# A planner's rule: a group already filled past 0.9 takes no further piece that costs more than 0.9

## The chip, the cores and the metric

The kernel runs on one core of a Trainium2 chip. The metric is the device time of one execution in microseconds (us), and the time of a kernel is the median of its runs. The engines are named as the profile names them: PE multiplies matrices, PEld is PE's loading of the stationary operand, DVE and POOL do elementwise work, ACT does activations and copies, SP issues transfers in the order of the program. Each engine works through its own list of instructions in order; semaphores tie the lists together.

## The reference

One post-norm transformer layer on x of 8 batches x 1024 rows x 256 columns, in float32:

```python
Q, K, V = (split_heads(x @ W.T + b) for W, b in ...)          # 16 heads of 16
scores = Q K^T / 4 + prior_lambda * gaussian_mask             # two bells over |i - j|
x = layernorm(x + (softmax(scores) V) @ Wo.T + bo)
h = bitlinear(x, w_fc) + gate * (x @ v.T @ fast_b.T @ u.T)    # 256 -> 1024
x = layernorm(x + bitlinear(relu(h)**2, w_proj))              # 1024 -> 256
```

bitlinear rounds the weights to -1, 0 and 1 times a scale per row. The attention is full: 1024 x 1024 scores for each of 8 x 16 heads.

## The kernel before

**The main loop.** The attention is cut into 512 groups, 64 for each of the 8 batches (`for g in range(-LEAD, total + 1)`; `per_batch` is 64 and `total` is 512). A batch has 4 sets of 4 heads, a set has two halves of 512 queries, and a half is 8 groups, one for each block of 128 keys. So a pattern comes back every 16 groups, and I call g modulo 16 the position of a group. In the order of the program, group g does this:

- `exp_scores` twice (L698 on): four PE matmuls into a PSUM tile pair `e` (L714), each for one head. Where a block of keys lies near the queries, the prior's window is added to the first pair by four more PE matmuls (L724, "prior") and to the second by DVE (L737). ACT then takes the exponential (L738). `near(g)` says whether the block is near; I call groups near and far by it.
- the pieces of other work that the planner chose for this group (their PE part),
- `max_scores` for group g + 12 (L647): four PE matmuls into tiles `s`, of which DVE takes the row maximum (L659, 1.22 us each, two a group),
- the elementwise part of the chosen pieces (their `empty` functions: ACT copies, DVE and POOL work) and what was deferred to this group (`run_deferred`),
- `weigh` for group g - 1 (L753): eight PE matmuls of the exponentials by V.

The tiles `e` and `s` take turns in three PSUM slots, so a group can also be held by the chain e, exponential, s, maximum. The pieces share two halves of one PSUM bank (`misc`).

**The pieces.** `jobs_of(b)` makes for every batch one list of pieces: queries and keys of this and the next batch (`queries_keys`, L593, and the transfers `write_parts` L196 to L201), transposes of x (`transpose_x`, L540), values (`values`, L566), and the layer's rest for the batch before, in four chunks of 256 rows (`chunk`): `project` (L953, two a chunk), `turn` (L987, two), `low_rank` (L1000), `hidden` (L1027 and L1034, eight) and `output` (L1062), two output rows of tiles with two parts each. A part of an output is 8 pairs of weight loads and 128x256 matmuls. Each piece is a tuple: its cost as the planner sees it, its function, how many of the two `misc` halves it takes, and a test of whether it may run yet.

The costs are 0.22 for `transpose_x`, 0.86 for `values`, `queries_keys` and `project`, 0.23 for `turn`, 0.48 for `low_rank`, 0.6 for `hidden` and 0.93 for a part of an `output`. Part 0 of an output takes one half of the bank, and part 1 goes on in the same half.

For the very last batch `last_chunk` has the same kinds of pieces, with `project` at 1.3 (L1163); its list `own` is put behind the others from group 505 on.

**The planner.** In group g it takes pieces from the front of the list as long as one fits. A second part of an output that stands at the front of the list when a group begins is always taken first. `filled` is the cost taken so far. `spare` says how many groups are left over in this batch, by a count of the larger pieces; in the last batch, groups 448 on, it is 0.

```python
spare = left - groups_for(jobs) if g < total - per_batch else 0
while jobs and halves >= jobs[0][2] and ready(jobs[0]):
    cost = jobs[0][0]
    if g < per_batch: ...
    elif filled > 0.75 and not (spare < (-1 if near(g) else 2)):
        break
    cost, piece, room = jobs.pop(larger(jobs) if halves == 1 and g >= per_batch else 0)[:3]
    filled += cost
```

So a group filled past 0.75 takes more only where few groups are to spare. `larger` may bring a piece of 0.5 to 0.9 ahead of small ones.

**Transfers at the pieces' edges.** `fill_stack` (L298, called at every sixteenth group) copies the next set's queries and keys from DRAM into SBUF, eight transfers of 256 KB, on SP; SP's list also has the writes of `write_parts`, the rows of maxima (L684, L691) and x (L99). `normalize` and the layer norms are spread over groups by `defer`.

**The end.** After group 512 the attention's PSUM pools are closed and the remaining pieces run one after the other, each with its elementwise part at once. Two pieces `divide_last(1)` and the projections of chunks 2 and 3 are set between them by place in the list (`jobs[:1]`, `jobs[1:4]`, `jobs[4:7]`, `jobs[7:8]`, `jobs[8:]`).

Of the kernel before, what the change touches and what calls it, by code (L numbers as in the profile page):

```python
# [38 lines left out]
def tile_postln_layer(  # L39
# [263 lines left out]
    def fill_stack(G):  # L303

        assert made.get((G // NG, G % NG // 2)) == 2 * NHALF
        for pr in range(NP):
            for a in range(2):
                for name in "kq":
                    fill_one(name, G, pr, a, nc.sync)
# [20 lines left out]
    def load_later():  # L330
        nc.sync.dma_start(v_sb, v)
        nc.sync.dma_start(fb_sb, fast_b)
        nc.sync.dma_start(u_sb, u.rearrange("(c p) r -> p c r", p=P))
        nc.sync.dma_start(gate_c, gate.partition_broadcast(P))
        nc.sync.dma_start(bo_row, bo.partition_broadcast(P))
# [32 lines left out]
    def run_deferred(upto):  # L368
        due = [f for n, f in later if n <= upto]
        later[:] = [u for u in later if u[0] > upto]  # L370
        for f in due:
            f()
# [283 lines left out]
    def max_row(t, blk, out, name):  # L656

        junk = p1.tile([P, L], F32, tag="junk", name=f"junk_{name}")
        nc.vector.tensor_tensor_reduce(  # L659
            out=junk,  # L660
            in0=t.rearrange("p k n -> p (k n)"),
            in1=wide[:, LEFT - P * blk : LEFT - P * blk + L],
            scale=1.0,
            scalar=-3.0e38,
            op0=ALU.add,
            op1=ALU.max,
            accum_out=out,
        )
# [29 lines left out]
    def exp_scores(i):  # L698

        step, n = divmod(i, STEP)
        G, h = divmod(step, NHALF)
        n, pr = divmod(n, NP)
        blk = order[h][n]
        s = G % SLOTS
        t = se(f"e_{i}")
        first = blk * P - MARGIN
        lo, hi = max(first, HALF * h), min(first + WIN, HALF * (h + 1))
        near = lo < hi  # L710
        by_pe = near and pr == 0 and (hi - lo > MARGIN or G < NG)
        for a in range(2):
            rows = slice(0, P if a else P // 2 + 2)
            nc.tensor.matmul(  # L714
                t[:, a, :],
                stack["k", s, pr, a][rows, ts(blk, P)],
                stack["q", s, pr, a][rows, ts(h, HALF)],
                start=True,
                stop=not by_pe,
            )  # L720
        if by_pe:
            for a in range(2):
                for n in range(2):
                    nc.tensor.matmul(  # L724
                        t[:, a, lo - HALF * h : hi - HALF * h],
                        ident_r,
                        prior[:, n, lo - first : hi - first],
                        start=False,
                        stop=(n == 1),
                    )  # L730
        e = big(f"exp_{i}")

        def rest():
            if near and not by_pe:
                part = t[:, :, lo - HALF * h : hi - HALF * h]
                add = win[:, lo - first : hi - first].unsqueeze(1)
                nc.vector.tensor_add(part, part, add.to_broadcast([P, 2, hi - lo]))  # L737
            nc.scalar.activation(e, t.rearrange("p a n -> p (a n)"), AF.Exp)  # L738

        return e, rest  # L740
# [674 lines left out]
    def ready(u):  # L1415

        return len(u) < 4 or u[3]()

    def larger(jobs):

        for n, u in enumerate(jobs[:5]):
            if 0.5 < u[0] < 0.9 and u[2] == 1 and ready(u):
                return n
            if u[0] != 0.22:
                break
        return 0
# [9 lines left out]
    def near(g):  # L1436

        step, n = divmod(g, NB)
        h = step % NHALF
        lo, hi = order[h][n] * P - MARGIN, (order[h][n] + 1) * P + MARGIN  # L1440
        return lo < HALF * (h + 1) and hi > HALF * h

    def groups_for(jobs):

        return sum(1.0 if u[0] > 0.7 else 0.5 if u[0] > 0.5 else 0.0 for u in jobs)
# [24 lines left out]
    for g in range(-LEAD, total + 1):  # L1470

        now = g
        if g == -2:
            fill_stack(1)
            load_later()
        if 0 <= g < total and g % per_batch == 0:
            if g:
                assert not jobs
                jobs = [u for part in jobs_of(g // per_batch) for u in part]
        if g == total - 7:  # L1480

            old, jobs = jobs, []
            while old and old[0][0] > 0.1 and old[0][2] == 0:
                jobs.append(old.pop(0))
            while old:
                jobs += [own.pop(0), *old[:2]]
                old = old[2:]
            jobs, own = jobs + own, []
        if g > 0 and 2 * g % PER_G == 0 and 2 * g // PER_G + 1 < B * NG:
            fill_stack(2 * g // PER_G + 1)  # L1490
        if 0 <= g < total:
            es[g], exps = zip(*(exp_scores(i) for i in (2 * g, 2 * g + 1)))
            exps[0]()

        if rest is not None:
            max_row(*rest)
            rest = None
        if 0 <= g < total:
            exps[1]()

        halves, work, filled = 2, [], 0.0

        if g >= 0 and jobs and jobs[0][0] > 0.1 and jobs[0][2] == 0:
            filled, piece = jobs.pop(0)[:2]
            work.append(piece)
            halves -= 1

        done = g + LEAD - (1 if g < 0 else 2)
        if done >= 0 and done % QSTEP == QSTEP - 1 and done < total:
            work.append(lambda done=done: set_max(done // QSTEP))  # L1510
            halves -= 1
        if g < 0:

            n = g + LEAD + 1 - (done >= QSTEP - 1)
            upto = 14 * n // (LEAD - 1)
            if halves == 2:
                work += [early.pop(0)[1] for _ in range(len(early) - 14 + upto)]
        elif g < total:
            left = per_batch - 1 - g % per_batch
            if g == 0:  # L1520
                among = len(jobs)
            if g < per_batch:

                behind = len(jobs) > among * (1 - (g + 1) / (per_batch - 3))
            else:
# [4 lines that stand above are left out]
                if g < per_batch:  # L1530
                    if not (cost == 0.0 or behind):
                        break
                    behind = len(jobs) - 1 > among * (1 - (g + 1) / (per_batch - 3))
                elif filled > 0.75 and not (spare < (-1 if near(g) else 2)):
                    break
                cost, piece, room = jobs.pop(larger(jobs) if halves == 1 and g >= per_batch else 0)[:3]
                filled += cost
                halves -= room
                work.append(piece)
                if cost == 0.01:  # L1540
                    break
                if jobs and jobs[0][0] > 0.1 and jobs[0][2] == 0:
                    halves = 0
        empties = [piece() for piece in work] if g >= 0 else []
        if g + LEAD < total:
            pair, blk, pm = max_scores(g + LEAD)
            max_row(pair[0], blk, pm[:, 0:1], f"{g + LEAD}_0")
            if g < 0:

                empties = [piece() for piece in work]  # L1550
            rest = pair[1], blk, pm[:, 1:2], f"{g + LEAD}_1"
        for empty in empties:
            if empty is not None:
                empty()
        run_deferred(g)
        if g - 1 in es:
            weigh((g - 1) // NB, (g - 1) % NB, es.pop(g - 1))
# [82 lines left out]
```

## Time and profile before

| | |
|---|---|
| median of 3 runs | 2231.86 us (2230.23 to 2234.39) |
| profiled execution: its time | 2231.73 us |
| profiled execution: span from first to last instruction | 2229.9 us |
| PE busy | 2160.5 us, 97% |
| DVE, ACT, POOL busy | 1591.5, 1442.7, 902.7 us |
| mean granted PE clock | 0.992 |

The starts of L714's first matmul in each group cut the trace into groups. From group 128 on a group takes 3.5 to 5.6 us; a group of the same position with the same pieces mostly takes the same time within 0.02 us in batch after batch. A row of the view of stretches gives, for the time from A to B, the busy time of each engine, with the number of instructions in brackets, then the granted PE clock (1.00 is full), the share of the transfer engines, and GB/s. A PE row that is shorter than the stretch shows PE waiting. In the timeline, the bracket at the end of a line is the engine's idle time before it and what ended it.

### The profile page before, as it was taken

Reading aid. Unit: us, or ns where it says so; the run is one execution under the profiler, and the core shown is the slowest. Engines: PE = TensorE matmul, PEld = TensorE weight load, DVE = VectorE, ACT = ScalarE, POOL = GpSimd, SP = SyncE. Lnnn points to the kernel's source line nnn. Section 1 sums busy time; section 2 is a strip of 40 time slices with the busy share of each in tenths; the row PEclk is TensorE's granted clock in tenths of the full one; section 3 lists DMA queues with packets and bytes.
Section 4 is the critical chain, followed back from the end, with each engine's and each line's share of the span. In section 5 each row is a group of like instructions: output and inputs, shape, how many; then the busy total and the mean of one; then the engine's idle time right before and its main releaser. Section 6 shows DMA issues by size and latency. Waiting matters only on the chain.

```text
span 2229.9 us, 36851 instructions
## 1 busy us (share of the span) xinstructions
PE 2160.5 (97%) x13144; PEld 1258.9 (56%) x13144; DVE 1591.5 (71%) x2952; ACT 1442.7 (65%) x2155; POOL 902.7 (40%) x1024
## 2 busy tenths in 40 slices
PE   6999999999999999999999999999999999999997
PEld 3444445555555555556555555555655555555557
DVE  6777776777777776777777777677777777677736
ACT  2665566666666667666666667676666666666654
POOL 4133322445333453245533444335443345444444
PEclk8999999999999999999999999999999999999998
DMA  7433334123433224423333223421344321422010
GB/s 194 109 92 89 74 96 114 66 71 75 118 115 87 56 56 119 129 71 80 75 125 103 73 67 92 130 87 52 75 118 116 87 71 46 132 70 53 22 46 20
DMA packets 110572, 193.36 MB, mean 87 GB/s; under 512 B 21100, under 2 KB 50108, under 8 KB 110388
## 3 DMA queue, kind: packets, MB, share of 16 engines
q1 hardware_dynamic: 108972, 189.42, 30.8%
q8 instruction: 104, 1.70, 0.3%
q10 hardware_dynamic: 1416, 1.58, 0.2%
q14 instruction: 80, 0.66, 0.1%
HBM read 105.19 MB, written 85.69 MB: 86 GB/s over the span
## 4 chain that ended last, share of the span: by engine, by line
PE 82%; DVE 8%; POOL 1%; issue 1%; ACT 1%; DMA 1%; SPq 0%; POOLq 0%; DVEq 0%; ACTq 0%
PE e L714 22%; PE av L753 19%; PE s L647 15%; DVE junk L659 6%; PE e L724 5%; PE misc L1027 4%; PE misc L593 4%; PE misc L1062 4%; PE misc L953 2%; PE misc L566 2%; PE misc L1034 1%; ACT exp L738 1%; DVE st L911 1%; PE misc L987 1%; PE misc L540 0%
## 5 line engine op out<-in xcount | busy, mean ns | idle before, releaser
L659 DVE CUSTOM_DVE_ANT_0 junk<-s,wide 128x1024 f32<-128x1024 f32 x1024 | 1248.6, 1219 | 534.3 <-PE s L647 492.0
L738 ACT ACTIVATE exp<-e 128x1024 f32<-128x1024 f32 x1024 | 1027.6, 1025 | 622.4 <-PE e L724 376.3
L714 PE MATMUL e<-st_q,st_k 66*128 66x512 f32 (+1 forms) x2048 | 664.6, 425 | 0.6 <-ACT exp L738 0.3
L714 PEld LDWEIGHTS e<-st_q,st_k 66*128 66x128 f32 (+1 forms) x2048 | 324.1, 189 | 463.3 <-ACT exp L738 82.5
L753 PE MATMUL av<-exp,v 128*17 128x512 f32 x4096 | 540.8, 600 | 0.0
L647 PE MATMUL s<-st_k,st_q 64*128 64x512 f32 x2048 | 400.5, 447 | 43.7 <-DVE pm L659 26.7
L647 PEld LDWEIGHTS s<-st_k,st_q 64*128 64x128 f32 x2048 | 167.3, 185 | 179.5 <-DVE pm L659 66.7
L737 DVE TENSOR_TENSOR e<-e,wide 128x372 f32<-128x372 f32 (+2 forms) x376 | 190.8, 507 | 47.0 <-PE e L714 41.9
L1045 POOL TENSOR_TENSOR rl<-rl 128x512 f32<-128x512 f32 x112 | 116.6, 1041 | 250.8 <-ACT hi L1044 243.4
L724 PEld LDWEIGHTS e<-prior,ident_r 128*128 128x128 f32 x1056 | 159.7, 190 | 24.2
L753 PEld LDWEIGHTS av<-exp,v 128*17 128x17 f32 x4096 | 68.1, 95 | 185.6 <-issue 184.5
L724 PE MATMUL e<-prior,ident_r 128*128 128x244 f32 (+2 forms) x1056 | 157.7, 272 | 0.0
L1047 POOL TENSOR_TENSOR lo<-rl,hi 128x512 fp32r<-128x512 f32 x112 | 143.9, 1285 | 8.8
L576 POOL TENSOR_TENSOR v<-v,bv_row 128x256 f32<-128x256 f32 x64 | 43.8, 686 | 213.4 <-ACT v L575 213.4
L1082 POOL TENSOR_TENSOR r<-r,sp_row 128x256 f32<-128x256 f32 x56 | 41.2, 735 | 205.1 <-ACT r L1081 205.1
L1027 PE MATMUL misc<-xhi,wfT 128*128 128x256 f32 x448 | 116.0, 282 | 0.2 <-ACT fullq L608 0.2
L1027 PE MATMUL misc<-xlo,wfT 128*128 128x256 f32 x448 | 115.1, 280 | 0.0
L1062 PE MATMUL misc<-wpT,lo 128*128 128x256 f32 x448 | 111.7, 283 | 2.1 <-POOL lo L1047 2.1
L1062 PE MATMUL misc<-wpT,hi 128*128 128x256 f32 x448 | 113.8, 287 | 0.0
L613 POOL TENSOR_TENSOR twok<-fullk,twok 128x512 fp32r<-128x512 f32 x30 | 38.6, 1288 | 163.0 <-ACT twok L612 163.0
L1040 ACT ACTIVATE rl<-misc,s_fc 128x256 f32<-128x256 f32 x224 | 94.3, 475 | 0.2
L1062 PEld LDWEIGHTS misc<-wpT,lo 128*128 128x128 f32 x448 | 85.1, 190 | 6.3 <-POOL lo L1047 2.9
(241 smaller groups left out, 2353.8 us busy)
## 6 DMA issues: line engine op xcount, KB each, us to landing
st_k<-parts_k SPq DMA_DIRECT2D x128, 256.0 KB
st_q<-parts_q SPq DMA_DIRECT2D x124, 256.0 KB
parts_k<-twok SPq DMA_DIRECT2D x60, 512.0 KB
parts_q<-twoq SPq DMA_DIRECT2D x64, 256.0 KB
parts_q<-twoq SPq DMA_DIRECT2D x30, 512.0 KB
x<-in_L_attn_x_dram SPq DMA_DIRECT2D x16, 512.0 KB
raw_o<-avs SPq DMA_DIRECT2D x248, 32.0 KB
rec<-back SPq DMA_DIRECT2D x30, 256.0 KB
```

Source lines behind the costliest of these rows:

```text
L647: nc.tensor.matmul(pair[a][:, kh, :], stack["q", s, pr, a][rows, ts(blk, P)], stack["k", s, pr, a][rows, ts(kh, HALF)], start=True, stop=True,
L659: nc.vector.tensor_tensor_reduce(out=junk, in0=t.rearrange("p k n -> p (k n)"), in1=wide[:, LEFT - P * blk : LEFT - P * blk + L], scale=1. ...
L714: nc.tensor.matmul(t[:, a, :], stack["k", s, pr, a][rows, ts(blk, P)], stack["q", s, pr, a][rows, ts(h, HALF)], start=True, stop=not by_pe,)
L724: nc.tensor.matmul(t[:, a, lo - HALF * h : hi - HALF * h], ident_r, prior[:, n, lo - first : hi - first], start=False, stop=(n == 1),)
L737: nc.vector.tensor_add(part, part, add.to_broadcast([P, 2, hi - lo]))
L738: nc.scalar.activation(e, t.rearrange("p a n -> p (a n)"), AF.Exp)
L753: nc.tensor.matmul(av[32 * j : 32 * j + HD + 1, :], v_bufs[b % 2][:, blk, g * HG + j, : HD + 1], es[j // 2][:, ts(j % 2, HALF)], start=(n ...
L1027: nc.tensor.matmul(ph, wfT[:, dc, ts(hc, P)], st[k2][:, dc, :], start=(dc == 0 and k2 == "xhi"), stop=False,)
L1040: nc.scalar.activation(rl[:, ts(k, n)], ph, AF.Relu, scale=s_fc[:, hc : hc + 1])
L1045: nc.gpsimd.tensor_mul(rl, rl, rl)
L1047: sub(lo, rl, hi.bitcast(F32))
L1062: nc.tensor.matmul(py, st[k][:, hc, ts(i, P)], wpT[:, hc, :], start=(hc == 0 and k == "hi"), stop=(hc == NHC - 1 and k == "lo"),)
```

## The change

One condition is added to the planner's loop. It is reached where the two conditions before it did not end the loop. It ends the loop when the group is filled past 0.9, the piece at the front costs more than 0.9, and `spare` is over -4. Pieces over 0.9 are the parts of an output (0.93) and the last batch's projections (1.3).

```diff
                 elif filled > 0.75 and not (spare < (-1 if near(g) else 2)):
                     break
+                elif filled > 0.9 and cost > 0.9 and spare > -4:
+                    break
                 cost, piece, room = jobs.pop(larger(jobs) if halves == 1 and g >= per_batch else 0)[:3]
                 filled += cost
                 halves -= room
```

No instruction is added, removed or resized; pieces go to other groups. Written X for `transpose_x`, Q for `queries_keys`, V for `values`, P for `project`, T for `turn`, L for `low_rank`, H for `hidden`, O for a part of an output, M for the transpose of the maxima (`set_max`), the groups differ as follows, and all others are the same:

```
groups 137 to 151, and the same 64, 128, 192, 256 groups later (batches 2 to 6)
before  XOO XQ XQ Q  MV V V V PP XQ XQ XQ MQ XT V
after   XO  O  XQ XQ MQ V V V VP XP XQ XQ MQ XQ TV

groups 459 to 462     before  QOO O OM -      after  QO O MO O
groups 481 to 493     before  OO - TOO T ML HH HH P PH HH HO O M
                      after   O  O TO  O MT L  HH HH PP HH HH O OM
groups 507 to 511     before  PP P P TT L     after  P P P P TT
```

In the last row P costs 1.3. After group 512 the list before begins with H of chunk 0; after the change it begins with L, one piece more, so the pieces set between by place come one piece earlier: before `H | divide | H T T | divide | H H L | P P | H | P P | H H H`, after `L | divide | H H T | divide | T H H | P P | L | P P | H H H H`. From there on the order is the same.

## The prediction

> **What bounds the kernel now.** I read the page first: the busy row, the clock and the chain that ended last.
>
> ```profile
> span 2229.9 us, 36851 instructions
> PE 2160.5 (97%) x13144; PEld 1258.9 (56%) x13144; DVE 1591.5 (71%) x2952; ACT 1442.7 (65%) x2155; POOL 902.7 (40%) x1024
> PEclk8999999999999999999999999999999999999998
> PE 82%; DVE 8%; POOL 1%; issue 1%; ACT 1%; DMA 1%; SPq 0%; POOLq 0%; DVEq 0%; ACTq 0%
> ```
>
> PE is busy nearly throughout and is 82% of the chain; the clock falls only at both ends. A change that only moves PE work between groups can then win only where PE waits. So next I cut the trace into groups and looked at the view of stretches, group by group, where pieces move. In the first stretch, groups 137, 138, 140, 150 and 151:
>
> ```profile
> 615.88:620.78 4.90, 4.90 (x38) 3.33 (x34) 2.83 (x7) 3.31 (x6) 0.73 (x1) 1.00 0.12 28
> 620.78:625.09 4.31, 4.31 (x30) 2.49 (x27) 3.02 (x6) 2.85 (x5) 0.73 (x1) 1.00 0.00 0
> ...
> 628.96:633.05 4.09, 4.09 (x28) 2.32 (x25) 3.14 (x6) 2.57 (x4) 1.49 (x2) 1.00 0.96 316
> ...
> 669.84:673.76 3.92, 3.92 (x29) 2.23 (x25) 3.25 (x6) 2.88 (x5) 1.30 (x1) 1.00 0.05 12
> 673.76:677.74 3.98, 3.71 (x24) 1.89 (x20) 2.98 (x8) 2.31 (x3) 0.19 (x1) 1.00 0.69 265
> ```
>
> Full groups are PE from end to end. Group 137 with three pieces takes 4.90. The least that PE needs in a far group without pieces is about 4.90 - 2 x 0.95 - 0.22 = 2.8 (O is 8 matmuls 0.12 apart, X 0.22), and some 3.2 in a near one (4.31 less X and Q, 0.86). Group 151, with only V, should need 2.8 + 0.86 = 3.66 and takes 3.98: thin groups are held by the chain through DVE. The last batch, in groups 462, 481, 482, 483 and 493, has more of this:
>
> ```profile
> 1957.50:1961.51 4.01, 3.80 (x24) 1.74 (x20) 3.36 (x6) 2.05 (x2) 3.18 (x4) 1.00 0.03 9
> ...
> 2037.35:2042.46 5.11, 4.96 (x37) 3.20 (x33) 2.88 (x7) 3.10 (x5) 4.26 (x6) 1.00 0.61 127
> 2042.46:2046.40 3.94, 3.80 (x24) 1.74 (x20) 3.36 (x6) 2.05 (x2) 2.87 (x3) 1.00 0.00 0
> 2046.40:2051.32 4.92, 4.92 (x38) 3.34 (x34) 2.65 (x7) 2.31 (x3) 0.00 (x0) 1.00 0.01 3
> ...
> 2088.92:2092.42 3.50, 3.03 (x22) 1.25 (x18) 2.54 (x5) 2.23 (x4) 3.42 (x4) 1.00 0.00 0
> ```
>
> Groups 462 and 482 have no piece at all and still take 4.01 and 3.94, 0.7 to 0.8 over PE's need; overfull neighbours take 5.11 and 4.92. An O put into an empty near group costs little there: the view of stretches has near groups with one O at 4.18 and far ones at 3.73.
>
> **The change part by part.** No instruction is added, so I price a group by one with the same pieces at a like position.
>
> Batches 2 to 6, groups 137 to 151 each. 137 goes from XOO to XO: the nearest rows are TO far, 3.96 (group 473) and 4.06 (five groups), I take 4.03: -0.87. 138 goes from XQ 4.31 to O 4.17 (group 106): -0.14. 140 goes from Q 4.09 to XQ 4.32 (group 148): +0.23. 150 goes from XT 3.92 to XQ 4.31 (group 70): +0.39. 151 goes from V 3.98 to TV, which I put at 4.05, the XQ of group 71 at that position: +0.07. The others move by a piece but keep a like content (145 from PP to VP, 146 from XQ to XP, 4.33 in group 78): +0.01. Sum -0.31 a batch, -1.6 in five. What is won is slack of the thin groups 150 and 151. Bounds: -0.6 a batch if both lose all their slack (3.92 - 3.67 for XT and 3.98 - 3.66), and +0.25 if O in 138 or 151's T makes PE wait once for the maxima as group 135's O does (0.25). SP: the last Q of queries and keys comes one group later, in 141, so its three writes fall behind the rows of maxima (L684, L691), as they do at group 149: some 5.5 us later. That holds back `fill_stack`. The first reader is `s` of group 148. From the timeline the last issue and that reader, and from the view of stretches the end of the copies:
>
> ```profile
> 645.80 0.59 SPq L298 DMA_DIRECT2D st_q<-parts_q  x1
> ...
> 652.00:654.00 2.00, 2.00 (x14) 0.74 (x15) 1.23 (x2) 0.65 (x2) 1.43 (x2) 1.00 0.33 78
> 654.00:656.00 2.00, 2.00 (x14) 1.68 (x12) 1.90 (x3) 1.03 (x1) 0.00 (x0) 1.00 0.00 1
> ...
> 664.43 0.73 PE L647 MATMUL s<-st_k,st_q 64*128 64x512 f32 x4
> ```
>
> The transfers are over by 654, the reader comes at 664.4. The writes take 3 us (transfer engines busy from 636 to 639), so the eight copies would start at 645.5 in place of 642 and be over by 657 or 658: 6 us of cover remain, and I cost it at nothing. The x load of group 139 moves to 140, and its first use at 146 stays; 20 us lie between.
>
> Groups 459 to 462. 18.00 us before (5.56, 4.18, 4.25, 4.01). After: QO is 5.56 - 0.95 = 4.61, O near 4.18, MO 3.83 (group 93), O near 4.18: 16.80, -1.2. But the second O's layer-norm statistics (DVE 0.42 and 0.18) now fall into group 463, beside the two subtractions of TT (0.42 each), and 463 and 464 already wait for DVE. I give back 0.3 (half of the 0.6 of DVE work): -0.9, bounds -1.2 and -0.6.
>
> Groups 481 to 493. 55.07 before. After, in order: 3.73, 4.17, 4.03, 4.17, MT 3.85, L 4.15 (group 464: 4.17), 4.05, 4.05, PP 4.50, 4.39, 3.95, 4.19, OM 3.83: 53.06, -2.0. Bounds -2.5, if L's group costs 3.7, PE's need alone, and -1.4, if the statistics beside T and L cost all their 0.6.
>
> Groups 507 to 510. 16.70 before. After, each with one P: 3.80, 4.27, 3.80, 4.27 (rows of 509 and 508 before), 16.14: -0.55, while TT (0.45 on PE) goes to 511 and L out of it. In 511 the exponentials now stand ahead of TT's copies on ACT (0.37 each), so the last of them ends some 0.5 us sooner. Bounds -1.0 and 0.
>
> The end. From the start of group 511 the list began after 5.8 us, with H. Now it begins with L after some 5.1. Before, H H L stood between the last divide and P P, and L waited 1.30 us for xlo. Now T H H stand there, and the first P waits instead for o_last (DVE L898, 0.68): DVE has lo (POOL 1.04 behind ACT 0.63 behind H), xlo, then o_last in line, ready at about 11.7 where P wants it at 10.7. That is a wait of 1.0 in place of 1.30, and L then waits for nothing. Summed piece by piece from the rows (L 0.6, divide 0.8, H 0.6, T 0.22, P 1.7), P P L P P H is done at 18.55 instead of 19.65 us from 511's start: -1.1. Chunk 3's inversion on POOL also stands earlier against H, before its products: some -0.45 off the next wait, below. Together -1.5. Bounds: -3, with that wait gone, and 0, if P waits 2.12 for o_last and POOL gives nothing.
>
> Sum: 1.6 + 0.9 + 2.0 + 0.55 + 1.5 = 6.6. Against the profiled execution's own 2231.73 (span 2229.9 and 1.83 around it, 0.13 under the median) that is 2225.1.
>
> **The clock.** The last wait decides more than its length:
>
> ```profile
> 2186.25 0.58 PE L1201 MATMUL plow<-xlo,v_st 128*128 128x256 f32 x1 [2.12 <-DVE xlo L1192]
> 2182.17:2185.58 3.41, 1.64 (x12) 1.24 (x10) 3.41 (x4) 1.99 (x6) 2.54 (x2) 1.00 0.00 0
> 2185.58:2192.41 6.83, 6.16 (x29) 6.16 (x30) 2.82 (x7) 4.34 (x10) 1.96 (x2) 0.50 0.00 0
> ```
>
> With PE busy 1.64 of 3.41 us the granted clock went to 0.50 for the next 6.83 us, so up to 3.4 us of PE time are lost there; the next low_rank could not start before its xlo (2189.94), 2.2 us before its 2192.17. If the wait shrinks to 1.6 the clock may hold. [...]
>
> **The rivals.**
>
> 1. The clock holds at the end: 2.1 us more, 2223.0. For it: the wait there shortens by my own working. Against it: 2.12 tripped it, and the windows' phase is not known.
>
> 2. The slack is not won but moved. PE time is conserved where groups are full, and thin groups may be held by DVE as before: nothing in the five batches, -0.6 and -1.4 in the last batch, -0.55, and nothing at the end: 2229.2, within 0.2%. For it: DVE's share of groups 462 to 464 is 3.4 of 4.0. Against it: 482's PE need is 0.75 below its time.
>
> 3. Slower: the copies of `fill_stack` arrive after `s` of group 148 wants them, in each of five batches. It decides from 664.4 on, 10.5 us later than before, where I expect 3.5 to 4. Each us past that costs 5. Group 72 shows such a wait (8.7 us for st_k), followed by 6.83 us at half clock, so from a wait of about 2 us it would cost 2 + 3.4 in each of the five, 27 in sum: 2252.
>
> **How the numbers follow.** Forecast 0.54, rival 1 0.18, rival 2 0.22, rival 3 0.06. About 0.2%, 4.5 us, is what a measurement of this kernel can tell from no change, so faster is below 2227.4: the forecast and rival 1, 0.72. Same 0.22, slower 0.06. The range goes from 2220, where rival 1 meets the far bounds of the five batches (-1.4) and of the last one's groups (-1.25), to 2230.5, past rival 2 by 1.3, near the distance of the lowest run from the median (1.6).
>
> **What would show it.** After: groups 137 to 151 last 61.55 in place of 61.86; 459 to 462 16.8; 481 to 493 53.1; no row of some 5 us in 481 to 484; a wait of P for o_last in place of low_rank's 1.30; the span from group 511's start 69 in place of 70.6. Wrong would be: a wait of `s` for st_q or st_k at groups 148, 212, 276; near groups with O above 4.3; or a second half-clock stretch at the end.

## The result and the profile after

The changed kernel takes 2224.47 us, the median of 14 runs (2220.16 to 2230.06), and the kernel before 2231.15 us (14 runs, 2227.19 to 2237.01). The ratio is 0.9967 with a 95% interval of 0.9957 to 0.9977: 0.33% faster, where 0.30% was forecast. The profiled execution took 2222.77 us. Its page has these lines in the places of those shown before:

```profile
span 2221.0 us, 36863 instructions
PE 2155.5 (97%) x13144; PEld 1256.3 (57%) x13144; DVE 1590.4 (72%) x2952; ACT 1440.8 (65%) x2155; POOL 903.5 (41%) x1024
PEclk8999999999999999999999999999999999999998
PE 83%; DVE 7%; POOL 1%; DMA 1%; ACT 1%; issue 1%; SPq 0%; POOLq 0%; DVEq 0%; ACTq 0%
```

The first row counts 12 instructions more, but none of an engine's own: those counts, in the second row, are the same. Nothing in the shares tells the two kernels apart. PE's busy time fell by 5 us although its instructions are the same: a part of its waiting counts as busy (the empty group 482 had 3.80 us of PE before, and eight matmuls more bring it only to 4.18, in a run below). The view of stretches tells more. Here are groups 137, 138, 140, 150 and 151 of the changed kernel (from A to B, busy time of PE, PEld, DVE, ACT and POOL, granted clock, transfer share, GB/s):

```profile
614.61:618.55 3.94, 3.94 (x30) 2.36 (x27) 2.84 (x7) 2.92 (x5) 0.00 (x0) 1.00 0.14 35
618.55:622.72 4.17, 4.17 (x33) 2.64 (x29) 3.02 (x6) 2.31 (x3) 0.41 (x1) 1.00 0.00 0
626.57:630.89 4.32, 4.32 (x30) 2.50 (x26) 3.46 (x8) 2.93 (x5) 3.81 (x5) 1.00 0.41 156
667.71:672.02 4.31, 4.31 (x31) 2.49 (x27) 3.02 (x6) 2.73 (x5) 2.19 (x2) 1.00 0.48 173
672.02:676.07 4.05, 3.94 (x26) 2.05 (x22) 2.87 (x7) 2.88 (x4) 1.29 (x1) 1.00 0.31 117
```

Each came out within 0.1 us of the row that I had put in its place. The next rows are groups 462, 464, 481, 482, 483 and 493:

```profile
1952.60:1956.79 4.19, 4.19 (x33) 2.66 (x29) 3.46 (x8) 2.32 (x3) 2.22 (x3) 1.00 0.03 8
...
1960.77:1965.46 4.69, 3.77 (x28) 2.08 (x24) 3.87 (x10) 2.54 (x4) 2.53 (x4) 1.00 1.04 217
2033.11:2036.84 3.73, 3.73 (x28) 2.19 (x24) 2.87 (x7) 2.72 (x4) 3.13 (x4) 1.00 0.95 198
2036.84:2041.03 4.19, 4.19 (x33) 2.66 (x29) 3.14 (x6) 2.31 (x3) 2.89 (x4) 1.00 0.01 4
2041.03:2044.98 3.95, 3.95 (x31) 2.35 (x27) 2.47 (x5) 2.20 (x3) 1.13 (x2) 1.00 0.02 4
2081.88:2085.73 3.85, 3.85 (x30) 2.23 (x26) 2.47 (x5) 2.49 (x5) 2.73 (x3) 1.00 0.00 0
```

Group 462 holds an O now and takes 4.19 in place of 4.01 empty. Group 464 stands out: PE is busy for 3.77 of 4.69 us, and it took 4.17 before. And here are the whole stretches, groups 137 to 151, 459 to 462, 463 to 465, 481 to 493, 507 to 510, and from group 511 to the end, first of the kernel before and then of the changed kernel.

```profile
615.88:677.74 61.86, 61.59 (x366) 34.54 (x362) 44.14 (x80) 41.52 (x64) 18.55 (x23) 1.00 0.40 121
1943.51:1961.51 18.00, 17.45 (x113) 10.51 (x109) 12.74 (x25) 9.91 (x14) 8.36 (x11) 1.00 0.16 62
1961.51:1973.62 12.11, 11.71 (x78) 6.72 (x74) 9.65 (x20) 8.67 (x13) 3.38 (x4) 1.00 0.51 119
2037.35:2092.42 55.07, 53.61 (x339) 31.46 (x335) 38.70 (x75) 36.05 (x53) 29.24 (x33) 1.00 0.10 25
2142.56:2159.26 16.70, 16.61 (x88) 8.54 (x84) 6.35 (x18) 7.84 (x9) 7.96 (x14) 1.00 0.12 36
2159.26:2229.95 70.69, 55.42 (x380) 48.83 (x376) 42.06 (x90) 30.82 (x64) 28.20 (x40) 0.90 0.05 16
```

```profile
614.61:676.07 61.46, 61.35 (x366) 34.34 (x362) 43.80 (x79) 41.10 (x63) 18.38 (x22) 1.00 0.38 112
1939.99:1956.79 16.80, 16.80 (x114) 10.45 (x110) 12.35 (x25) 9.90 (x14) 7.06 (x10) 1.00 0.17 65
1956.79:1969.41 12.62, 11.70 (x78) 6.71 (x74) 10.00 (x20) 8.66 (x13) 4.74 (x6) 1.00 0.86 194
2033.11:2085.73 52.62, 52.07 (x339) 31.30 (x335) 38.91 (x75) 35.27 (x53) 28.64 (x32) 1.00 0.12 29
2135.75:2152.05 16.30, 16.18 (x85) 8.04 (x81) 5.98 (x16) 8.34 (x9) 7.25 (x12) 1.00 0.12 37
2152.05:2220.99 68.94, 54.80 (x384) 48.36 (x380) 41.36 (x93) 30.24 (x63) 29.51 (x42) 0.90 0.05 16
```

| stretch | before, us | after, us | change | forecast |
|---|---|---|---|---|
| groups 137 to 151 and four repeats | 5 x 61.86 | 61.47, 61.50, 61.46, 61.50, 61.50 | -1.9 | -1.6 |
| groups 459 to 462 | 18.00 | 16.80 | -1.2 | -1.2 |
| groups 463 to 465 | 12.11 | 12.62 | +0.5 | +0.3 |
| groups 481 to 493 | 55.07 | 52.62 | -2.4 | -2.0 |
| groups 507 to 510 | 16.70 | 16.30 | -0.4 | -0.55 |
| from group 511 on | 70.7 | 68.9 | -1.7 | -1.5 |

That is -7.1 us. The two spans differ by 8.9 us. Of the other 1.8 us, 1.3 lie ahead of group 137, where both kernels have the same order: groups 0 to 63 took 254.3 before and 252.8 after, groups 72 and 73 12.3 and 10.8, and the time ahead of group 0 was 1.2 us longer after. In the profiles of the experiments below, whose order ahead of group 137 is also the same up to there (all but the one that moves the copies), these stretches lie anywhere from 252.8 to 255.9 and from 9.3 to 12.7 us. So that difference is between executions and not the change's.

### The profile page after: what moved, and what is told of

It reads as the page before. It is cut to its first block, busy times and chain, and to the rows that moved or that the text cites. A ratio compares the mean times of both kernels' runs of the same rounds, so it can differ in the third digit from the quotient of the medians.

```text
span 2221.0 us, 36863 instructions
## 1 busy us (share of the span) xinstructions
PE 2155.5 (97%) x13144; PEld 1256.3 (57%) x13144; DVE 1590.4 (72%) x2952; ACT 1440.8 (65%) x2155; POOL 903.5 (41%) x1024
## 4 chain that ended last, share of the span: by engine, by line
PE 83%; DVE 7%; POOL 1%; DMA 1%; ACT 1%; issue 1%; SPq 0%; POOLq 0%; DVEq 0%; ACTq 0%
PE e L714 22%; PE av L753 19%; PE s L647 15%; DVE junk L659 5%; PE e L724 5%; PE misc L1027 4%; PE misc L1062 4%; PE misc L593 4%; PE misc L566 2%; PE misc L953 2%; PE misc L1034 1%; PE misc L987 1%; ACT exp L738 1%; DVE st L911 1%; PE misc L540 0%
```

## The experiments

Three theories were set against each other. A, slack: PE's work costs its own time in every full group, and what is won is PE's waiting in thin groups. B, overfull: a group with two large pieces costs more than its pieces apart, so the gain goes with the number of pairs that are pulled apart. C, the end: most comes from the last batch's projections and the list's new order behind group 512. A's figures for the first three runs are those of the changed kernel's own trace, so what these runs can show is that the parts stand alone and add up. What tells A from B is the fourth run, on the cost of a piece.

**One part at a time.** The first run keeps the condition to batches 2 to 6:

```diff
-                elif filled > 0.9 and cost > 0.9 and spare > -4:
+                elif filled > 0.9 and cost > 0.9 and spare > -4 and g < total - per_batch:
```

> The added condition holds in batches 2 to 6 alone (groups 128 to 447), and the last batch is planned as before. Theory A (slack): PE work costs its own time in every full group, and all that is won is PE's waiting in thin groups. Then groups 137 to 151 and their four repeats last 61.5 each in place of 61.86, 1.9 us in sum, nothing else moves by over 0.3 us, and the time is about 0.1% under the kernel before. Theory B (overfull): a group with two large pieces costs more than its pieces apart, so the gain goes with the number of pairs pulled apart. The nine pairs of the changed kernel brought 5.4 us in the groups, 0.6 each, and the five pairs here bring 3.0. Theory C (the end): most of the gain is at the end and in the last batch's projections, and this run is within 0.5 us of the kernel before.

The ratio is 0.9991 (0.9982 to 1.0), which just reaches no change. In the trace the five stretches last 61.44 to 61.46 us, 2.06 us less in sum, and 459 to 493 are as before (18.00, 12.09 and 55.08 us). The gain is A's 1.9, not B's 3.0, and not C's zero.

The second keeps it to the outputs of the last batch:

```diff
-                elif filled > 0.9 and cost > 0.9 and spare > -4:
+                elif filled > 0.9 and 1 > cost > 0.9 and spare > -4 and g >= total - per_batch:
```

> The added condition holds for the outputs of the last batch alone; batches 2 to 6 and the projections at 1.3 are as before. Theory A: groups 459 to 465 give 0.7 us (1.2 less in 459 to 462, 0.5 more in 464), groups 481 to 493 give 2.4, sum 3.1, because 462, 482 and 493 stood empty; the end from group 507 on is as before within 0.5 us. Theory B: three pairs pulled apart, 1.8 us. Theory C: under 0.5 us.

The ratio is 0.9988 (0.9979 to 0.9997). Groups 459 to 462 take 16.78, 463 to 465 12.63, and 481 to 493 52.65: -3.1 us, A's number, where B has 1.8. Three pairs pulled apart give more than five did in the middle, as here they fill groups that stood empty.

The third keeps it to the projections at 1.3:

```diff
-                elif filled > 0.9 and cost > 0.9 and spare > -4:
+                elif filled > 0.9 and cost > 1 and spare > -4:
```

> The added condition holds for the projections at 1.3 alone, so only groups 507 to 511 and the order of the list after group 512 change. Theory A: the end wins 2.1 us (0.4 in groups 507 to 510, 1.7 from group 511's start on) because the waits in it are fewer: 0.95 for o_last in place of 1.30 and 0.49 for xlo. Theory B: one pair, 0.6 us in 507 to 510 and nothing after. If the end's 1.7 came from an accident of the clock, it is not seen again here.

The ratio is 0.9993 (0.9984 to 1.0002), which holds no change too. In the trace groups 507 to 510 take 16.27 (-0.43), and the end takes 68.87 us from group 511's start, as in the changed kernel. But the profile of the kernel before is a poor base for that number: the two runs above and the next one all have the end of the kernel before, and theirs lasts 69.59, 69.78 and 69.85, not 70.69. In the profile of the kernel before the clock stayed at 0.50 for 6.83 us behind the wait for xlo (what xhi leaves of x, a subtraction on DVE), in these three and in the changed kernel for 3.4 us. So about 0.9 us of the 1.7 was that one profile's clock, and the order is worth some 0.7 to 1.0. A measure that this clock does not touch says the same: the matmul that waits for xlo starts 26.99 to 27.01 us after group 511's start in the four profiles with the end of before, and 26.13 or 26.14 in the changed kernel and in this run, 0.86 less.

The three ratios add up to 0.28% and the whole measured 0.33%, the same within their intervals.

**What a piece costs in a full and in an empty group.** The kernel before, with 8 matmuls more in four groups:

```diff
+        if g in (142, 143, 462, 482):
+            for hc in range(NHC):
+                nc.tensor.matmul(
+                    two_halves[:, 1 - last_half[0], :], wpT[:, hc, :P], wpT[:, hc, :],
+                    start=(hc == 0), stop=(hc == NHC - 1),
+                )
```

> The kernel before with 8 matmuls more (128x256, of wpT by itself, into the half of the misc bank that is free; the result is not read) in groups 142 and 143, which have one V each and are full, and in 462 and 482, which have no piece. 8 such matmuls need 0.95 us of PE. Theory A: 142 and 143 go from 4.10 to 5.05, and 462 and 482 from 4.01 and 3.95 to about 4.2, so 0.2 each. Theory B, in which the second large piece in a group is what costs: about 0.95 or more in 142 and 143, and the same 0.95 in the empty ones as PE work is never free.

The view of stretches of this run, groups 142, 143, 462 and 482:

```profile
638.23:643.28 5.05, 5.05 (x37) 3.42 (x33) 3.14 (x6) 2.42 (x3) 1.11 (x2) 1.00 0.37 139
643.28:648.31 5.03, 5.03 (x36) 3.40 (x32) 3.02 (x6) 2.42 (x3) 0.69 (x1) 1.00 0.67 143
1960.69:1964.88 4.19, 4.19 (x33) 2.66 (x29) 3.14 (x6) 2.05 (x2) 3.17 (x4) 1.00 0.04 10
2045.74:2049.92 4.18, 4.18 (x32) 2.65 (x28) 3.13 (x6) 2.05 (x2) 2.87 (x3) 1.00 0.00 0
```

In the full groups the eight matmuls cost 0.95 and 0.94 us, all of their PE time; in the empty ones 0.18 and 0.24. The groups behind them (144, 463 and 483: 4.09, 3.98 and 4.89) changed by 0.03 at most. That is A by itself, for PE's part of a piece: work moved from a full group into an empty near one wins 0.95 and pays 0.2. What a piece costs on the other engines is not in this run, whose eight matmuls have no elementwise part. Its one execution took 2237.27 us, beside 2232.99 of the kernel before.

**Why group 464 got slower.** My reason was the second O's layer-norm statistics on DVE beside the two subtractions of TT. In the trace PE's wait for the maxima in this group is longer than before (first line before, second line after):

```profile
1968.02 0.73 PE L647 MATMUL s<-st_k,st_q 64*128 64x512 f32 x4 [0.40 <-DVE pm L659]
...
1963.82 0.73 PE L647 MATMUL s<-st_k,st_q 64*128 64x512 f32 x4 [0.92 <-DVE pm L659]
```

The changed kernel with these statistics three groups later:

```diff
-                defer(1, measure)
+                late = 3 if now == 462 else 0
+                defer(1 + late, measure)
                 if i == CT - 1:
-                    defer(2, finish)
+                    defer(2 + late, finish)
```

> The changed kernel, with the layer norm's statistics (0.42 and 0.18 us of DVE) and the normalisation behind the last O of group 462 put three groups later, to 466 and 467. If those statistics beside the two subtractions of TT are what makes L's group 464 wait (4.69 in place of 4.17 before), 464 falls back to 4.15 to 4.25 and groups 463 to 465 last 12.1 in place of 12.63; the statistics cost at most 0.1 in 466, a full group. If the wait has another cause (463 begins later against the maxima because 462 is full), it stays at 4.6 or more.

Group 464 of this run:

```profile
1962.37:1966.54 4.17, 3.77 (x29) 2.09 (x25) 3.37 (x8) 2.54 (x4) 0.00 (x0) 1.00 1.03 218
```

It is back at 4.17, and groups 463 to 465 take 12.09. By the trace DVE now does the statistics at the start of group 467; 466 and 467 take 4.40 and 4.50, as in the changed kernel. So the cause is shown: DVE busy 3.87 in the changed kernel against 3.37 here, and the 0.5 went straight to PE's wait for the maxima (0.92 against 0.40).

**The end's order.** Two runs set the divides and projections at other places of the end's list. The first goes back to the order of before, behind L:

```diff
-    jobs = [*jobs[:1], last[0], *jobs[1:4], last[1], *jobs[4:7], *e2["P"], *jobs[7:8], *e3["P"], *jobs[8:]]
+    jobs = [*jobs[:2], last[0], *jobs[2:5], last[1], *jobs[5:8], *e2["P"], *jobs[8:9], *e3["P"], *jobs[9:]]
```

> The changed kernel, but the two divides and the projections are set one place later in the end's list, so that behind L the order is that of the kernel before: L H, divide, H T T, divide, H H L, P P, H, P P, H H H. If the order made the end shorter, as I worked out (P waits 0.95 for o_last in place of L's 1.30 for xlo, and one H more stands behind the last P), the time from group 511's start goes from 68.9 to about 70.2. If only what stands in group 511 counts (exponentials ahead of the copies), it stays at 68.9.

The end takes 71.30 us and the ratio is 0.9986 (0.9976 to 0.9995). That is 2.4 us more than in the changed kernel, in the direction that the order would have it, but this run does not measure the order alone: in its profile the clock was at 0.50 from 2164.7 on for 3.4 us more, at most 1.7 us of PE's time, which leaves 0.7 or more. The waits themselves, from PE's timeline of this run, are other ones than I expected, 0.51 for low and 0.47 for xlo in place of one of 1.30:

```profile
2163.90 0.39 PE L1247 MATMUL ph<-low,lowT 128*128 128x256 f32 x1 [0.51 <-DVE low L1217]
...
2170.02 0.72 PE L1201 MATMUL plow<-x,v_st 128*128 128x256 f32 x3 [0.47 <-DVE x L1192]
...
2185.47 0.58 PE L1201 MATMUL plow<-xlo,v_st 128*128 128x256 f32 x1 [2.14 <-DVE xlo L1192]
```

The second puts the last divide behind the first H:

```diff
-    jobs = [*jobs[:1], last[0], *jobs[1:4], last[1], *jobs[4:7], *e2["P"], *jobs[7:8], *e3["P"], *jobs[8:]]
+    jobs = [*jobs[:1], last[0], *jobs[1:2], last[1], *jobs[2:7], *e2["P"], *jobs[7:8], *e3["P"], *jobs[8:]]
```

> The changed kernel, but the last divide stands behind the first H: L, divide, H, divide, H T T H H, P P, L, P P, H H H H. o_last then stands ahead of lo and xlo in DVE's list and is ready by the time P wants it, so the 0.95 us wait goes: 68.9 from group 511's start becomes 68.0. Rival: DVE's xlo and lo come 0.7 later each, the later wait of low_rank for xlo (2.05) grows by as much, and the sum stays at 68.9; or a new wait for recs stands before the divide, 0.5.

PE's waits in the end of this run:

```profile
2162.12 0.66 PE L895 MATMUL precs<-ident,recs 128*128 128x128 f32 x4 [0.24 <-DVE recs L885]
...
2180.23 0.38 PE L1201 MATMUL plow<-xlo,v_st 128*128 128x256 f32 x1 [2.19 <-DVE xlo L1192]
```

P's 0.95 us for o_last is gone, 0.24 for recs is new, and the wait for xlo grew from 2.05 to 2.19. The end takes 68.56 in place of 68.94, and the matmul on xlo starts 25.71 us after group 511's start in place of 26.14: 0.4 of the 0.95, so both the theory and its rival hold in part. The ratio is 0.9975 (0.9962 to 0.9987).

**Both mends together.** The later statistics and the early divide in one kernel:

```diff
+                late = 3 if now == 462 else 0
...
-    jobs = [*jobs[:1], last[0], *jobs[1:4], last[1], *jobs[4:7], ...
+    jobs = [*jobs[:1], last[0], *jobs[1:2], last[1], *jobs[2:7], ...
```

> The changed kernel with the later statistics and with the divide behind the first H, as in the run before this one at the end: 0.4 us less at the end, and 0.5 less in groups 463 to 465 if that cause holds, so about 0.9 us under the changed kernel and 0.35 to 0.4% under the kernel before. This is too little to tell from the changed kernel by the times; the stretches in the trace have to show it.

Groups 463 to 465 take 12.08 and the end 68.49, 1.0 us less than in the changed kernel. The ratio to the kernel before is 0.9969 (0.9957 to 0.998): 0.31% faster, where 0.35 to 0.4% was expected, and by the times not to be told from the changed kernel, as expected.

**The slower rival.** The changed kernel with `fill_stack` one group later for every set:

```diff
-        if g > 0 and 2 * g % PER_G == 0 and 2 * g // PER_G + 1 < B * NG:
+        if g > 1 and 2 * (g - 1) % PER_G == 0 and 2 * g // PER_G + 1 < B * NG:
             fill_stack(2 * g // PER_G + 1)
```

> The changed kernel with the copies of fill_stack called one group later for every set. In SP's list they then stand behind the five transfers of raw_o and sums, which wait for the exponentials' sums, so at group 144 they start at about +8.5 us from the group's start in place of +0 and end at about +18.5 or +19. The first s that reads them comes at +19.4. If the cover was as I read it (9 us left in the changed kernel), s waits 0 to 1 us in each of the sets, and the time rises by under 15 us over 28 sets, most likely by under 5. If the changed kernel already stood at the edge of rival 3, each set waits 5 us or more and the clock halves behind it: over 100 us.

It took 2308.97 us in its one run, beside 2231.78 of the kernel before: 77 us slower, and some 84 above the changed kernel's median. But `s` of group 148 did not wait. From the timeline of this run, the first and the last copy at group 144 (SP) and the reader (PE), 2.7 us into group 148 as in the changed kernel:

```profile
678.89 0.50 SPq L298 DMA_DIRECT2D st_k<-parts_k  x1
...
683.26 0.59 SPq L298 DMA_DIRECT2D st_q<-parts_q  x1
...
691.14 0.74 PE L647 MATMUL s<-st_k,st_q 64*128 64x512 f32 x4
```

The copies start 7.2 us after the group's own start (671.70) where they start 3.6 us ahead of it in the changed kernel, and the reader still has no wait in its bracket. Behind the start of the kernel no wait of PE in this run is put down to these copies. The cost came in another way. The wait for s that PE shows at group 132 (3.89 us) is put down to DVE, and DVE's timeline there says why:

```profile
616.80 1.22 DVE L659 CUSTOM_DVE_ANT_0 junk<-s,wide 128x1024 f32<-128x1024 f32 x1 [1.35 <-PE s L647]
617.96 0.08 DVE L659 DVE_READ_ACCUMULATOR2_ANT pm<- 128x1 f32 x1
622.40 0.55 DVE L796 RECIPROCAL den<-den 128x64 f32<-128x64 f32 x1 [4.37 <-DMA den<-sums]
```

The small transfer of the softmax sums (den, 32 KB) now stands behind the eight copies in SP's list, and its data, it seems, behind theirs. DVE's reciprocal waits for it, and the maxima queue behind the reciprocal. In the list of DVE's waits of this run:

```profile
DVE den L796 <- DMA den<-sums: 51.9, 13, 7.2
```

13 waits, 51.9 us in sum; the changed kernel has none. That the issue comes later is not all of it: in the changed kernel the reciprocal runs as soon as 3.8 us after the issue without a wait, and here it never runs sooner than 7.0 us after it. The 13 groups with such a wait lost 2.9 to 8.0 us against the changed kernel, and the group behind, at half clock behind most of them, up to 1.6 more, some 67 us together. Sets without a normalisation, such as the one at 144, lost nothing, but for two other transfers that also stand behind the copies here: DVE waited 7.34 us for the load of the projection weights (`proj`), and group 52 lost 8.7; and DVE waited 3.42 for POOL, which sat idle until a load of x, and groups 469 to 471 lost 7.2.

## Why the prediction was right, step by step

- **The sum**: some of it is luck. Forecast were 6.6 us. With the end counted at the 0.86 of the clock-free measure the stretches give 6.3: the end's miss of 0.6 and the 0.2 of group 464 are partly set off by 0.3 and 0.4 more in batches 2 to 6 and in groups 481 to 493.
- **Pricing by like groups** held. The largest miss of a group that I priced by a row is 0.3 us (485, MT, 3.55 where I took 3.85).
- **Batches 2 to 6**, -1.6: right in sign and mechanism; the size was -1.9, since XO took 3.94 and not 4.03.
- **`fill_stack` at nothing**: right. In the changed kernel its second copy, which reads what the writes bring, starts at 641.98, 2.1 us later against group 144 than before (I had 3.5); the copies are over by 653, and `s` reads at 662.3.
- **Groups 459 to 462 and 463**: -1.2 exactly. What I gave back for DVE, 0.3, was 0.5, nearly all of the 0.6 us of statistics. I halved it for no reason in the trace; PE already waited 0.40 for DVE there, and that wait grew by 0.52. That is the term mis-sized.
- **Groups 481 to 493**, -2.0: -2.4. Here TT is split, and by the trace DVE does the statistics in groups 484 and 486, each time beside one subtraction in place of two. They cost next to nothing: PE waits 0.25 for the maxima in 485 and 0.17 in 486, MT took 3.55 and L 3.98.
- **Groups 507 to 510**, -0.55: -0.4.
- **The end**, -1.5: the 1.7 of the two profiles hides a miss. Against the three runs with the old end and the same length of half clock it is some -0.8. The first of its two terms, -1.1, came out at -0.78: the matmul on xhi ahead of the wait for xlo starts 23.70 us after group 511's start in place of 24.48. The wait of P for o_last came as worked out (0.95 for 1.0) and L's was gone, but P wanted o_last at 11.07 and had it at 12.02, where I had 10.7 and 11.7. The second term, -0.45 from POOL's earlier inversion, did not come: the wait for xlo is 2.05 in place of 2.12. That is the step that failed. POOL's three products (L1261) begin only 0.28 us earlier against that matmul on xhi, as the first now waits for ACT's hi, and the profile has them take 4.33 us in place of 3.71 (spans on POOL are rough). So DVE now waits for POOL three times before it comes to xlo.

DVE's timeline has this, first of the kernel before and then of the changed kernel:

```profile
2182.07 0.69 DVE L1262 TENSOR_TENSOR lo<-rl,hi 128x512 fp32r<-128x512 f32 x1 [1.76 <-POOL rl L1261]
...
2183.73 1.52 DVE L1262 TENSOR_TENSOR lo<-wide,hi 128x512 fp32r<-128x512 f32 x1
2185.18 0.68 DVE L1262 TENSOR_TENSOR st_k<-rl,st_q 128x512 fp32r<-128x512 f32 x1
...
2173.85 0.69 DVE L1262 TENSOR_TENSOR lo<-rl,hi 128x512 fp32r<-128x512 f32 x1 [0.93 <-POOL rl L1261]
2175.48 0.69 DVE L1262 TENSOR_TENSOR lo<-wide,hi 128x512 fp32r<-128x512 f32 x1 [0.93 <-POOL wide L1261]
2177.10 0.69 DVE L1262 TENSOR_TENSOR st_k<-rl,st_q 128x512 fp32r<-128x512 f32 x1 [0.93 <-POOL rl L1261]
```

Before, DVE waited once and then worked without a pause, its second lo taking 1.52 us in place of 0.69. Why the same instructions of DVE and POOL take longer in one place than in another was not found out.

PE's timeline of the changed kernel has the two waits:

```profile
2164.07 0.70 PE L1163 MATMUL po<-wo_last,o_last 128*128 128x256 f32 x2 [0.95 <-DVE o_last L898]
...
2178.18 0.39 PE L1201 MATMUL plow<-xlo,v_st 128*128 128x256 f32 x1 [2.05 <-DVE xlo L1192]
```

And its view of stretches has the window of the second wait and the one behind it:

```profile
2175.90:2179.33 3.43, 1.38 (x10) 1.15 (x11) 2.05 (x5) 1.93 (x6) 2.21 (x2) 1.00 0.00 0
2179.33:2182.75 3.42, 3.42 (x19) 3.42 (x18) 1.46 (x4) 2.30 (x6) 0.11 (x1) 0.50 0.00 0
```

- **Rival 1, the clock holds**: fell. In the traces of the two kernels every stretch at one granted clock, but for the last, which ends with the span, lasts 3.41 us or a whole multiple of it; I call 3.41 us a window. PE was busy for 1.38 of 3.43 us, and the next window ran at 0.50. So it was in all eleven profiles, with PE busy for 1.1 to 1.6 us of the window that holds the wait for xlo. Before, a window with PE busy for 2.12 of 3.42 us, the one with L's 1.30, was followed by full clock; in the run with the order of before one with 2.22 was not. The half clock lasted one window here (3.41 us) and two in the profile of before (6.83 us); why two was not found out, and no run shows what sets the clock.
- **Rival 2, slack only moved**: fell for the groups. It was half right at the end.
- **Rival 3, the copies late**: did not come, and the mechanism is further off than I had it: copies some 9 us later still than in the changed kernel did not hold `s` up at group 148. Its price came from a misreading: the 8.7 us wait for st_k is at 25.78 us, ahead of group 0. In group 72 PE waits 1.53 us for ACT's exponential, and ACT had waited 2.66 for a transfer of `parts_k`. That a late transfer in that queue turned out to cost about as much is luck: the readers held up are those of the softmax sums and of two loads, not of the copies, as far as this one run shows.

## What to carry to other kernels

Where one engine is busy throughout, cut the trace into the units that repeat and read each one's time against its content: what a move is worth is the waiting in the thin units, and full units give back what they are relieved of (here eight matmuls more cost 0.95 and 0.94 us in full groups, and 0.18 and 0.24 in empty ones). Price a unit by one with the same content elsewhere in the trace; here that gave the sum within a few tenths of a us for each stretch of groups. Where a thin unit already waits for a second engine, count that engine's share of the moved work in full; here 0.5 of 0.6 us came through. Where the units end, as behind group 512, the same care is needed for each engine in the chain: here the engine that was taken to be ready earlier was so by 0.28 us and then took longer, by the profile 4.33 us in place of 3.71.

## What was not expected of the hardware

A 32 KB transfer issued behind eight copies of 256 KB kept DVE waiting for 3.1 to 4.8 us in twelve sets, and for 7.2 in one; on the trace the cost appears as PE waiting for the maxima, and only DVE's own waits name the transfer. And executions of one and the same order differ in fixed places: groups 72 and 73 took from 9.3 to 12.7 us, and the half clock behind the wait for xlo lasted 3.4 or 6.8 us. Spans of two single profiles therefore cannot be subtracted at the level of 2 us, while the stretch of groups 137 to 151 agrees within 0.1 us wherever its order is the same.
